# Top-p attention and adjacency on one core: sums from counts, two adj accumulators, layer 1's weights in two pieces

## The chip, the cores and the metric

The kernel runs on one core of a Trainium2 chip. The metric is the device time of that core, in microseconds (us); lower is better. The core has five engines with instruction streams of their own: TensorE (PE in the profile; its weight loads are PEld), VectorE (DVE), ScalarE (ACT), GpSimd (POOL), and SyncE (SP), which here only issues DMAs. They meet through semaphores. Each engine works through its stream in order.

## The reference, cut to what matters

There are N = 3327 nodes with 256 features; `adj` is a sparse random matrix with weights, held dense. Two layers follow each other; only the first concerns us closely.

```python
h  = relu(layernorm(x))
R  = (adj + I) / rowsum
for n in range(2):                      # two propagation steps
    A  = top_p(softmax(q @ k.T), 0.9)   # q, k: 64 wide, from Xa
    Xf = R @ Xf
    Xa = A @ Xa
    Z  = Z + Xf @ U1[n].T + Xa @ U2[n].T
x  = x + layernorm(h + Z) * g + b
# layer 1: attention over neighbours (4 heads of 64), masked by adj > 0
x  = x + elu(softmax(mask(leaky_relu(s_i + d_j))) @ (relu(layernorm(x)) @ W))
```

`top_p` keeps, in each row, the largest probabilities until they sum to 0.9, and sets the others to zero. Put the other way: it drops the smallest entries whose sum stays below 0.1 of the row's sum.

## The kernel before, in words

The 3327 rows make 26 tiles of 128 rows (NT = 26). Layer 0 goes through two propagation steps (n = 0 and n = 1, called the first and the second step here). Per step and row tile there are two streams of work.

**Attention rows** (class `Row`, pieces put by `search` and `attention`). Logits come from TensorE (L842), their exponentials from ScalarE (L853), which leaves a row of 3327 float32 numbers `e` in SBUF. Then the threshold is sought without a sort. A guess t0 comes from the row's moments. At a threshold t the kernel needs twice the sum of all entries below t, called B, and compares it with b, a tenth of the row's sum. `count` (L890) makes it with two passes of ScalarE over the row: Relu(t - e) summed gives `r0`, Sign(t - e) summed gives `s0` (the number below less the number above), and B = (s0 + N) t - 2 r0. `step` (L904 and after) takes B, estimates the density near t and moves to the next threshold by a damped Newton step; it is a string of some fifteen operations on one number per row, on GpSimd for the first two thresholds. The first step of propagation uses two thresholds, the second three (`EVALS`). At the third, VectorE makes the sum in one pass (`sum_below`, L936) and also does the `step`. After it VectorE takes the largest entries below the last threshold (`window`, L947 and L952), sorts them and finds the exact cut (`sort`, `choose`), and sets what is below it to zero (`drop`, L1002). A window of 24 or 32 entries must hold the cut; `least` is a guard that opens the window fully when few entries are left above the threshold. TensorE then transposes the row, 128 columns at a time (L1015), ScalarE copies the transposes to SBUF (`et`, L1020), and TensorE multiplies them with Xa into the accumulator `acca` (L1027).

**Adjacency tiles** (class `Full`, put by `full`). 26 blocks of adj come by DMA into `at` buffers (L1047) and are multiplied on TensorE into one accumulator `accf` in PSUM (L1053), two blocks to a planned piece. ScalarE copies the result out (`copy`, L1060), and VectorE adds it up (`add`, L1069 and after). There is one accumulator, so tile t+1 can't begin before the copy of tile t.

**Layer 1's weights** (`layer1_weights`, L700): four loads and eight VectorE operations, in one piece put with `plan.put("DVE", 3.0, base + NT - 1.0, layer1, needs=[used], lag=3.0)`. It needs only the first projections (`used`). Two tiles of the `et` pool, which has three, hold its data; the planner isn't told of these.

**The order of the work** is set by a planner written in the kernel, `Plan` (L470 and after). Every piece of work has an engine, an assumed length, a rank, needs (pieces that must be done), and buffers that it takes and gives. `order` plays the pieces through on assumed clocks: whenever an engine is free, it starts the ready piece of lowest rank whose buffers are free. Each engine's stream stands in that order, for good; on the chip the engines follow it and wait on semaphores where the data aren't there. A wait that the planner doesn't know of, or a length that it assumes too short, doesn't change the order. The ScalarE copies of accumulators have rank -90 and so come as early as ScalarE is free in the plan. `Row.count` on ScalarE is assumed to take 3.05, `Row.step` on GpSimd 3.8 and 4.7, `sum_below` on VectorE 3.65.

Layer 1 (`attend_neighbours`) follows from about 1775 us on and is not touched; its two kinds of accumulators use the PSUM space of `acca` and `accf`.

Of the kernel before, what the change touches and what calls it, by code (L numbers as in the profile page):

```python
# [10 lines left out]
F32 = mybir.dt.float32  # L11
BF16 = mybir.dt.bfloat16
I32 = mybir.dt.int32
U16 = mybir.dt.uint16
AF = mybir.ActivationFunctionType
ALU = mybir.AluOpType
# [3 lines left out]
P = 128  # L20
N = 3327
NT = 26
NP = NT * P
D = 256
# [7 lines left out]
BIG = 3.0e38  # L32
# [13 lines left out]
WIN = (24, 32)  # L46
# [6 lines left out]
BUFS = dict(kk=2, e=4, sc=6, f=3, xa=2, xt=2, kq=3, ystage=2, base=1, mv=4, cum=2)  # L53
# [517 lines left out]
def fast(  # L571
# [18 lines left out]
    V, S, T, GP = nc.vector, nc.scalar, nc.tensor, nc.gpsimd  # L590
# [35 lines left out]
    with ExitStack() as l0:  # L626
# [3 lines left out]
        scr = l0.enter_context(tc.tile_pool(name="scr", bufs=1))  # L630
# [3 lines left out]
        ps_a = l0.enter_context(tc.tile_pool(name="ps_a", bufs=1, space=PSUM))  # L634
# [62 lines left out]
                for r in range(2):  # L697
                    S.copy(wqk[:, k, r, (1 - r) * DA : (2 - r) * DA], ps)

        def layer1_weights():  # L700

            late = wpool.tile([P, 2 * D + 2 * (H * FH + 2 * H)], F32, name="late")
            g_all, b_all = late[:, :D], late[:, D : 2 * D]
            wa = late[:, 2 * D :].rearrange("p (c o) -> p c o", c=2)
            a_all = etpool.tile([P, H, 2 * FH], F32, name="et")
            nc.sync.dma_start(g_all, ln_g.partition_broadcast(P))
            nc.sync.dma_start(b_all, ln_b.partition_broadcast(P))
            nc.sync.dma_start(a_all, gat_a.partition_broadcast(P))
            nc.sync.dma_start(wa[:, :, : H * FH], gat_w.rearrange("(c p) o -> p c o", p=P))
            prod = etpool.tile([P, 2, H, FH], F32, name="et")  # L710
            for k in range(2):
                for a in range(2):
                    V.tensor_mul(
                        prod[:, 0],
                        wa[:, k, : H * FH].rearrange("p (h f) -> p h f", h=H),
                        a_all[:, :, a * FH : (a + 1) * FH],
                    )
                    lo = H * FH + a * H
                    V.tensor_reduce(wa[:, k, lo : lo + H], prod[:, 0], AX.X, ALU.add)
            return g_all, b_all, wa  # L720

        def moments(t, kq, ps_k, ps_g):

# [84 lines left out]
            a = plan.put("ACT", 0.6, rank, exps, needs=[a])  # L808
            return plan.put("DVE", 0.6, rank, rest, needs=[a])

        plan = Plan(dict(pl=2, px=2, acca=1, accf=1, et=3, at=4, y=1, e2=2, mask=2, **BUFS))

        class Row:


            NAMES = (
                "b v w t0 t1 t2 u g k2 p0 p1 p2 p3 j0 j1 j2 j3 r0 s0 B0 B1 B2 q d dt least up h0 h1 room K zs nxt cnt m "
                "tk rec".split()
            )

# [64 lines left out]
            def count(self, k, fn):  # L885

                junk = scr.tile([P, NP], mybir.dt.float8e5, name="junk")
                dst = (self.r0, self.s0)[fn == AF.Sign]
                t = (self.t0, self.t1, self.t2)[k]
                S.activation(junk[:, :N], self.e[:, :N], fn, bias=t, scale=-1.0, accum_out=dst, saturate=False)  # L890

            def step(self, k, eng):

                TS, TT = eng.tensor_scalar, eng.tensor_tensor
                t, tn, B = (self.t0, self.t1, self.t2)[k], (self.t1, self.t2, self.up)[k], (self.B0, self.B1, self.B2)[k]
                last = k + 1 == EVALS[self.n]

                def invert(x):
                    if eng is V:
                        V.reciprocal(x, x)  # L900
                    else:
                        TT(x, x, powers[:, 2:3], ALU.pow)

                if k < 2:  # L904
                    TS(self.q, self.s0, float(N), t, ALU.add, ALU.mult)  # L905
                    TS(B, self.r0, -2.0, self.q, ALU.mult, ALU.add)
                else:
                    TS(B, B, 2.0, None, ALU.mult)
                TS(self.d, B, -0.5, self.b, ALU.mult, ALU.add)
                if k == 0:  # L910

                    TS(self.g, self.u, cs[:, self.i : self.i + 1], 0.25, ALU.mult, ALU.min)
                    TS(self.least, self.s0, N - 2.0 * (WIN[self.n] - 2), BIG, ALU.is_ge, ALU.mult)
                    TS(self.least, self.d, 0.0, self.least, ALU.is_ge, ALU.mult)
                else:
                    TT(self.u, B, (self.B0, self.B1)[k - 1], ALU.subtract)
                    TT(self.w, self.k2, self.g, ALU.mult)
                    TS(self.w, self.u, self.dt, self.w, ALU.mult, ALU.add)
                    TS(self.v, self.u, self.u, self.k2, ALU.mult, ALU.add)
                    invert(self.v)  # L920
                    TT(self.g, self.w, self.v, ALU.mult)
                TS(self.q, self.g, 0.5, 1.0 / AIM[self.n], ALU.mult, ALU.add)
                invert(self.q)
                TS(self.d, self.q, t, self.d, ALU.mult, ALU.add)  # L924
                TT(self.d, self.d, self.g, ALU.mult)
                if last:
                    TS(self.d, self.d, t, self.least, ALU.add, ALU.max)
                    TS(self.up, t, 0.25, self.d, ALU.mult, ALU.max)  # L928
                else:
                    TT(self.d, self.d, t, ALU.add)  # L930
                    TS(tn, t, 0.25, self.d, ALU.mult, ALU.max)  # L931
                    TS(self.dt, tn, t, 2.0, ALU.subtract, ALU.mult)

            def sum_below(self):
                y = scr.tile([P, NP], BF16, name="y")
                V.scalar_tensor_tensor(  # L936
                    y[:, :N], self.e[:, :N], self.t2, self.e[:, :N], ALU.is_lt, ALU.mult, accum_out=self.B2
                )

            def window(self, a, part):  # L940

# [95 lines left out]
        class Full:  # L1037


            def __init__(self, n, t):  # L1040
                self.n, self.t, self.at = n, t, {}
                self.src, self.w = (main, D + 1) if n == 0 else (c, D)

            def load(self, q):
                m = min(JC, NT - q * JC)
# [2 lines left out]

            def some(self, js):
                for j in js:  # L1050
                    if j == 0:
                        self.acc = ps_a.tile([P, D + 1], F32, name="accf")
                    T.matmul(  # L1053
                        self.acc[:, : self.w], self.at[j // JC][:, j % JC, :], self.src[:, j, : self.w],
                        start=(j == 0), stop=(j == NT - 1),
                    )
# [286 lines left out]
        def search(row, rank, keys, stats_of, fresh):  # L1343


            n, i = row.n, row.i
            got, a = [], None
# [14 lines left out]
            a = plan.put("ACT", 0.35, rank - 2.4, row.row_sum, needs=[got])  # L1362
# [1 line left out]
            a = row.pieces["guess"] = plan.put("ACT", 1.0, rank - 2.4, row.guess, needs=[a])  # L1364
            more = plan.put("ACT", 0.85, rank - 2.05, row.density, needs=[a])
            for j in range(2):
                got = [plan.put("ACT", 3.05, rank - (2.1, 1.7)[j], row.count, j, fn, needs=[a]) for fn in (AF.Relu, AF.Sign)]
                a = plan.put("POOL", (3.8, 4.7)[j], rank - (2.0, 1.6)[j], row.step, j, GP, needs=[got, more])
            if EVALS[n] == 3:
                a = plan.put("DVE", 3.65, rank - 1.3, row.sum_below, needs=[a], take=["y"], give=["y"], lag=0.02, hold=3.6)  # L1370
                a = plan.put("DVE", 2.7, rank - 1.3, row.step, 2, V, needs=[a])
            halves = []
            for h in range(2):
# [33 lines left out]
        def full(n, t, rank, right, after):  # L1407

            f = Full(n, t)
            loads = [  # L1410
                plan.put("SP", 0.1, rank, f.load, q, needs=[after], take=["at"], lag=3.3) for q in range(-(-NT // JC))
            ]
            loaded[0] = loads[-1]
            a = None
            for j in range(0, NT, 2):
                last = j % JC == JC - 2 or j == NT - 2
                a = plan.put(
                    "PE", 0.437 * 2, rank, f.some, range(j, j + 2), needs=[a, loads[j // JC], right[j : j + 2]],
                    take=["accf"] * (j == 0), give=["at"] * last,
                )  # L1420
            a = plan.put("ACT", 0.3, -90.0, f.copy, needs=[a], take=["f"], give=["accf"])
            if n == 1:
                b = plan.put("SP", 0.1, rank, f.fetch, needs=[loads[-1], stored[t]], take=["base"], lag=3.0)
                return plan.put("DVE", 0.88, -90.0, f.add, needs=[a, b], give=["f", "base"], hold=0.85)
            return plan.put("DVE", 1.15, -90.0, f.add, needs=[a], give=["f"])
# [229 lines left out]
        layer1_ready = None  # L1655
        sources = [project_u(t, -1.9 + 0.001 * t) for t in range(NT)]
        right, fresh, failed = None, None, []
        for n in range(STEPS):
            base = 30.0 * n
# [21 lines left out]
            if n == 0:  # L1681
# [13 lines left out]
                used, sources = sources, [(p,) for p in fulls]  # L1695

                def layer1():
                    late["g"], late["b"], late["wa"] = layer1_weights()

                layer1_ready = plan.put("DVE", 3.0, base + NT - 1.0, layer1, needs=[used], lag=3.0)  # L1700
            else:
                ends = [finish2(r, done[r.i], fulls[r.i], base + r.i + 0.2) for r in rows]
        attend_neighbours(rows, ends, done, fulls)
# [62 lines left out]
```

## Time and profile before

The time is the median of three runs.

| | |
|---|---|
| time, median (lowest to highest) | 2310.74 us (2310.22 to 2312.15) |
| span of the profiled run, clock | 2307.9 us, 0.988 |
| ScalarE counts, L890 | 208 x 3072 ns, and 191 ns each to read the sum |
| VectorE sums at the third threshold, L936 | 26 x 3672 ns, and 83 ns each |
| adj matmuls, L1053 | 1352 x 383 ns (first step), 1352 x 388 ns (second step) |
| copy of the adj accumulator, L1060 | 52 x 368 ns |
| layer 1's weights on VectorE, L713 and L719 | 4 x 425 ns, 4 x 420 ns |

In time: up to about 120 us the inputs are read and projected; the first step runs to about 970 us, the second to about 1775 us, and layer 1 to the end. Lines of the profile give a group of instructions by source line, engine and operation; a wait is written as who waited, then after an arrow for whom, with the total in us, the number of times, and the longest. In a list in order of time the brackets hold the idle time of that engine before the instruction, and what ended it. Idle time of an engine that doesn't set the end costs nothing.

### The profile page before, as it was taken

The page shows a single profiled execution, that of the slowest core. Times are in us where ns is not written, and L with a number is a line of the kernel's source. Part 1 is how long each engine was busy: PE and PEld are TensorE (multiplying, and loading weights), DVE is VectorE, ACT ScalarE, POOL GpSimd, SP SyncE. Part 2 cuts the span into 40 slices and gives each one's busy share as a digit, 9 for nine tenths or more (in the row PEclk, how much of TensorE's full clock was granted, in tenths as well). Part 3 has the DMA queues.
Part 4 walks back from the last instruction along what each step waited for, and adds up shares of the span by engine and source line. Part 5 has one row for each costly group of instructions (what it writes and reads, how often), then busy time and mean ns, then how long its engine had stood idle before and what let it go on. Part 6 is the DMA issues. An engine that isn't in the chain of part 4 may idle for free. (4 is left out here: it accounts for less than half of the span.)

```text
span 2307.9 us, 36154 instructions
## 1 busy us (share of the span) xinstructions
PE 2223.0 (96%) x11956; PEld 1551.9 (67%) x11956; DVE 1699.8 (74%) x4299; ACT 1559.9 (68%) x2901; POOL 1017.6 (44%) x2263
## 2 busy tenths in 40 slices
PE   7989999999999999999999999999998999999997
PEld 5467777777877778777777778777877434333332
DVE  5564666656645664389889889889888797989895
ACT  5767788678777862488676787777773556565553
POOL 6345455445554541357766765677774000000000
PEclk9999999999999999999999999999999999999998
DMA  3021212212212222522212222122223343434341
GB/s 97 1 68 52 68 54 60 64 53 61 73 47 72 68 87 73 176 85 65 65 51 68 68 76 67 53 62 68 71 67 99 90 114 109 116 99 127 100 130 42
DMA packets 189654, 176.97 MB, mean 77 GB/s; under 512 B 14866, under 2 KB 145808, under 8 KB 189328
## 3 DMA queue, kind: packets, MB, share of 16 engines
q1 hardware_dynamic: 187472, 173.30, 25.8%
q8 instruction: 96, 1.57, 0.3%
q10 hardware_dynamic: 1984, 1.26, 0.2%
q14 instruction: 102, 0.84, 0.1%
HBM read 157.66 MB, written 15.89 MB: 75 GB/s over the span
## 5 line engine op out<-in xcount | busy, mean ns | idle before, releaser
L890 ACT ACTIVATE junk<-e,sc 128x3327 fp8e5<-128x3327 f32 x208 | 638.9, 3072 | 25.4 <-POOL sc L931 23.4
L1027 PE MATMUL acca<-rhs,et 128*128 128x256 f32 x2704 | 623.6, 381 | 2.3 <-ACT et L1020 2.2
L1027 PEld LDWEIGHTS acca<-rhs,et 128*128 128x128 f32 x2704 | 500.6, 191 | 66.9 <-ACT et L1020 4.8
L1053 PE MATMUL accf<-c,at 128*128 128x256 f32 x1352 | 322.8, 388 | 20.4 <-ACT f L1060 20.3
L947 DVE SCALAR_TENSOR_TENSOR y<-e,sc 128x1664 f32<-128x1664 f32 x104 | 204.6, 1967 | 187.0 <-POOL sc L928 169.3
L1053 PE MATMUL accf<-main,at 128*128 128x257 f32 x1352 | 317.0, 383 | 4.8 <-DMA at<-in_adjt_dram 4.5
L1020 ACT COPY et<-px 128x512 f32<-128x512 f32 (+1 forms) x364 | 194.4, 554 | 186.4 <-PE acca L1027 125.3
L1053 PEld LDWEIGHTS accf<-c,at 128*128 128x128 f32 x1352 | 251.6, 192 | 78.4 <-ACT f L1060 28.8
L1522 DVE SCALAR_TENSOR_TENSOR e<-c,low,et 128x832 f32<-128x832 f32 x288 | 289.1, 1075 | 16.8 <-ACT e L1592 9.5
L1053 PEld LDWEIGHTS accf<-main,at 128*128 128x128 f32 x1352 | 250.9, 191 | 46.4 <-issue 8.0
L952 DVE MAX8 cands<-y 128x8 f32<-128x208 f32 x832 | 241.1, 361 | 3.6
L1002 DVE SCALAR_TENSOR_TENSOR e<-e,thr 128x832 f32<-128x832 f32 x208 | 214.0, 1083 | 2.6 <-ACT kq L1178 0.5
L1538 PE MATMUL pl<-e,main 128*64 128x416 f32 x1152 | 212.6, 516 | 0.1
L1015 PE MATMUL px<-ident,e 128*128 128x128 f32 x1352 | 196.4, 277 | 16.8 <-ACT et L1020 7.9
L853 ACT ACTIVATE e<-pl 128x1024 f32<-128x1024 f32 x208 | 179.3, 865 | 45.6 <-PE pl L842 44.7
L1015 PEld LDWEIGHTS px<-ident,e 128*128 128x128 f32 x1352 | 163.4, 143 | 57.5 <-issue 13.6
L1511 ACT ACTIVATE et<-at 128x512 bf16<-128x512 f32 (+1 forms) x208 | 114.5, 550 | 118.3 <-DVE e L1522 76.9
L842 PE MATMUL pl<-kt,qq 64*128 64x512 f32 (+1 forms) x728 | 184.1, 588 | 0.0
L905 POOL TENSOR_SCALAR sc<-sc 128x1 f32<-128x1 f32 x104 | 40.2, 386 | 309.3 <-ACT junk L890 249.3
L1538 PEld LDWEIGHTS pl<-e,main 128*64 128x64 f32 x1152 | 79.6, 137 | 123.1 <-issue 104.0
L936 DVE SCALAR_TENSOR_TENSOR y<-e,sc 128x3327 bf16<-128x3327 f32 x26 | 95.5, 3672 | 47.9 <-POOL sc L931 47.9
L1522 DVE SCALAR_TENSOR_TENSOR rhs<-c,low,et 128x832 f32<-128x832 f32 x128 | 129.2, 1073 | 0.0
(485 smaller groups left out, 3076.8 us busy)
## 6 DMA issues: line engine op xcount, KB each, us to landing
at<-in_adjt_dram SPq DMA_DIRECT2D x416, 256.0 KB, 2.8
at<-in_adjt_dram SPq DMA_DIRECT2D x104, 192.0 KB, 3.0
at<-in_adjt_dram SPq DMA_DIRECT2D x52, 128.0 KB, 2.1
ys<-ystage SPq DMA_DIRECT2D x26, 256.0 KB, 2.4
rhs<-in_x_dram SPq DMA_DIRECT2D x26, 128.0 KB, 3.3
ystage<-in_x_dram SPq DMA_DIRECT2D x26, 128.0 KB, 2.1
base<-ys SPq DMA_DIRECT2D x26, 128.0 KB, 2.2
x1s<-ystage SPq DMA_DIRECT2D x26, 128.0 KB, 1.7
```

The source lines that it names most:

```text
L842: T.matmul(pl[:, r, :m], qq[half, self.i, :], kt[half, 512 * k : 512 * k + m], start=True, stop=True,)
L853: S.activation(self.e[:, 1024 * k : 1024 * k + pl.shape[1]], pl, AF.Exp, accum_out=(self.p0, self.p1, self.p2, self.p3)[k],)
L890: S.activation(junk[:, :N], self.e[:, :N], fn, bias=t, scale=-1.0, accum_out=dst, saturate=False)
L947: V.scalar_tensor_tensor(self.y[:, : hi - lo], self.e[:, lo:hi], self.up, self.e[:, lo:hi], ALU.is_lt, ALU.mult, accum_out=(self.h0, self. ...
L952: V.max(self.cands[:, o // PIECE, :], self.y[:, o - lo : min(o + PIECE, hi) - lo])
L1002: V.scalar_tensor_tensor(piece, piece, self.thr[:, o : o + 1], piece, ALU.is_gt, ALU.mult)
L1015: T.transpose(pt[:, k, :], self.e[:, j * P : (j + 1) * P], ident)
L1020: S.copy(self.et[g][:, :m, :], self.pt.pop(g)[:, :m, :])
L1027: T.matmul(self.acc, et[:, j - 4 * g, :], rhs[self.n][:, j, :], start=(j == 0), stop=(j == NT - 1))
L1053: T.matmul(self.acc[:, : self.w], self.at[j // JC][:, j % JC, :], self.src[:, j, : self.w], start=(j == 0), stop=(j == NT - 1),)
L1522: V.scalar_tensor_tensor(held["e"][:, k, :], extra["both"][b % 2][:, k, :], low[:, j, k : k + 1], held["mask"], ALU.max, ALU.mult,)
L1538: T.matmul(q["acc"][a][k * FH : (k + 1) * FH, c, :C], main[:, j, h * FH : (h + 1) * FH], held["e"][:, h, c * C : (c + 1) * C], start=(j == 0),
```

## The change

It has three parts.

**Sums from counts.** Between two neighbouring thresholds t_(k-1) and t_k lie (s_k - s_(k-1)) / 2 entries; each is taken to be worth the mean of the two thresholds. So twice the sum changes by (s_k - s_(k-1)) (t_k + t_(k-1)) / 2, and only the Sign count is needed at the second and third threshold. The Relu pass at the second threshold goes in both steps, and the VectorE pass at the third is replaced by a Sign pass on ScalarE. The counts need columns of their own (`s0 s1 s2`). The guard `least` is computed at threshold k = n instead of always at the first.

**Two adj accumulators in the second step.** One PSUM tile of 2 x 256 float32 numbers holds two accumulators; tiles of even and odd number take them in turn. The planner knows them as `accf0` and `accf1`, and holds `accf` itself for the whole step.

**Layer 1's weights in two pieces.** The loads are a piece on the DMA queue that needs row 3's attention to be done and takes an `et` buffer; the VectorE operations are a second piece that needs the loads and takes another.

```diff
-        def layer1_weights():
+        def layer1_loads():
...
+            return g_all, b_all, wa, a_all
+
+        def layer1_scores(wa, a_all):
+
             prod = etpool.tile([P, 2, H, FH], F32, name="et")
...
-                dst = (self.r0, self.s0)[fn == AF.Sign]
+                dst = (self.s0, self.s1, self.s2)[k] if fn == AF.Sign else self.r0
...
-                if k < 2:
-                    TS(self.q, self.s0, float(N), t, ALU.add, ALU.mult)
+                s = (self.s0, self.s1, self.s2)
+                if k == 0:
+                    TS(self.q, s[0], float(N), t, ALU.add, ALU.mult)
                     TS(B, self.r0, -2.0, self.q, ALU.mult, ALU.add)
                 else:
-                    TS(B, B, 2.0, None, ALU.mult)
+                    TS(self.q, t, (self.t0, self.t1)[k - 1], 0.5, ALU.add, ALU.mult)
+                    TS(self.u, s[k], s[k - 1], self.q, ALU.subtract, ALU.mult)
+                    TT(B, (self.B0, self.B1)[k - 1], self.u, ALU.add)
                 TS(self.d, B, -0.5, self.b, ALU.mult, ALU.add)
+                if k == self.n:
+
+                    TS(self.least, s[k], N - 2.0 * (WIN[self.n] - 2), BIG, ALU.is_ge, ALU.mult)
+                    TS(self.least, self.d, 0.0, self.least, ALU.is_ge, ALU.mult)
                 if k == 0:
-
                     TS(self.g, self.u, cs[:, self.i : self.i + 1], 0.25, ALU.mult, ALU.min)
-                    TS(self.least, self.s0, N - 2.0 * (WIN[self.n] - 2), BIG, ALU.is_ge, ALU.mult)
-                    TS(self.least, self.d, 0.0, self.least, ALU.is_ge, ALU.mult)
                 else:
-                    TT(self.u, B, (self.B0, self.B1)[k - 1], ALU.subtract)
...
-                    if j == 0:
+                    if j == 0 and self.n == 0:
                         self.acc = ps_a.tile([P, D + 1], F32, name="accf")
+                    elif j == 0:
+
+                        if self.t == 0:
+                            late["accf"] = ps_a.tile([P, 2, D], F32, name="accf")
+                        self.acc = late["accf"][:, self.t % 2, :]
...
-                got = [plan.put("ACT", 3.05, rank - (2.1, 1.7)[j], row.count, j, fn, needs=[a]) for fn in (AF.Relu, AF.Sign)]
+                got = [
+                    plan.put("ACT", 3.05, rank - (2.1, 1.7)[j], row.count, j, fn, needs=[a])
+                    for fn in (AF.Relu, AF.Sign)[j:]
+                ]
                 a = plan.put("POOL", (3.8, 4.7)[j], rank - (2.0, 1.6)[j], row.step, j, GP, needs=[got, more])
             if EVALS[n] == 3:
-                a = plan.put("DVE", 3.65, rank - 1.3, row.sum_below, needs=[a], take=["y"], give=["y"], lag=0.02, hold=3.6)
+                a = plan.put("ACT", 3.05, rank - 1.4, row.count, 2, AF.Sign, needs=[a])
                 a = plan.put("DVE", 2.7, rank - 1.3, row.step, 2, V, needs=[a])
...
-                    take=["accf"] * (j == 0), give=["at"] * last,
+                    take=[f.bank] * (j == 0) + ["accf"] * (n == 1 and t + j == 0), give=["at"] * last,
                 )
-            a = plan.put("ACT", 0.3, -90.0, f.copy, needs=[a], take=["f"], give=["accf"])
+            a = plan.put(
+                "ACT", 0.3, -90.0, f.copy, needs=[a], take=["f"],
+                give=[f.bank] + ["accf"] * (n == 1 and t == NT - 1),
+            )
...
-                layer1_ready = plan.put("DVE", 3.0, base + NT - 1.0, layer1, needs=[used], lag=3.0)
+                a = plan.put("SP", 0.5, base + 4.0, layer1, needs=[used, done[3]], take=["et"], lag=8.0)
+                layer1_ready = plan.put(
+                    "DVE", 3.7, base + 5.0, lambda: layer1_scores(late["wa"], late["a"]), needs=[a], take=["et"],
+                    give=["et", "et"],
+                )
```

More of the change, by code (lines that the diff above doesn't have):

```diff
@@ L719, in layer1_weights @@
                     V.tensor_reduce(wa[:, k, lo : lo + H], prod[:, 0], AX.X, ALU.add)
-            return g_all, b_all, wa
         def moments(t, kq, ps_k, ps_g):
@@ L809, in stats @@
             return plan.put("DVE", 0.6, rank, rest, needs=[a])
-        plan = Plan(dict(pl=2, px=2, acca=1, accf=1, et=3, at=4, y=1, e2=2, mask=2, **BUFS))
+        plan = Plan(dict(pl=2, px=2, acca=1, accf=1, accf0=1, accf1=1, et=3, at=4, y=1, e2=2, mask=2, **BUFS))
         class Row:
             NAMES = (
-                "b v w t0 t1 t2 u g k2 p0 p1 p2 p3 j0 j1 j2 j3 r0 s0 B0 B1 B2 q d dt least up h0 h1 room K zs nxt cnt m "
+                "b v w t0 t1 t2 u g k2 p0 p1 p2 p3 j0 j1 j2 j3 r0 s0 s1 s2 B0 B1 B2 q d dt least up h0 h1 room K zs nxt cnt m "
                 "tk rec".split()
@@ L932, in step @@
                     TS(self.dt, tn, t, 2.0, ALU.subtract, ALU.mult)
[L934 to L938, printed above, removed]
             def window(self, a, part):
@@ L1042, in __init__ @@
                 self.src, self.w = (main, D + 1) if n == 0 else (c, D)
+                self.bank = f"accf{t % 2}" if n else "accf"
             def load(self, q):
@@ L1697, in layer1 @@
                 def layer1():
-                    late["g"], late["b"], late["wa"] = layer1_weights()
-                layer1_ready = plan.put("DVE", 3.0, base + NT - 1.0, layer1, needs=[used], lag=3.0)
+                    late["g"], late["b"], late["wa"], late["a"] = layer1_loads()
+                a = plan.put("SP", 0.5, base + 4.0, layer1, needs=[used, done[3]], take=["et"], lag=8.0)
[3 more added lines that the diff above has]
+                )
             else:
```

## The prediction

> **What bounds the kernel now.** I read the page's busy times and its forty slices first, then the stretches of the two propagation steps, then TensorE's waits in the second step, and last the order in time around its longest gaps.
>
> ```profile
> PE 2223.0 (96%) x11956; PEld 1551.9 (67%) x11956; DVE 1699.8 (74%) x4299; ACT 1559.9 (68%) x2901; POOL 1017.6 (44%) x2263
> ...
> PEclk9999999999999999999999999999999999999998
> ```
>
> TensorE sets the time; whatever is won must be TensorE idle time, or time at a reduced clock. Idle altogether: 2307.9 - 2223.0 = 85 us. The stretches say where (columns: length; then busy time of TensorE, its weight load, VectorE, ScalarE, GpSimd; then the clock):
>
> ```profile
> 100.00:150.00 50.00, 40.03 (x156) 25.45 (x157) 36.50 (x129) 35.26 (x60) 19.68 (x54) 0.93 0.12 37
> ...
> 150.00:800.00 650.00, 648.41 (x3195) 509.59 (x3193) 383.61 (x1137) 499.59 (x827) 337.26 (x802) 1.00 0.21 61
> 1000.00:1750.00 750.00, 726.03 (x3550) 582.82 (x3549) 654.78 (x1885) 563.98 (x953) 530.76 (x1068) 0.99 0.23 67
> ```
>
> The body of the first step (150 to 800) has 1.6 us of idle: nothing can be won there. The body of the second has 24 us, with VectorE at 87% against 59% in the first. Before 150 us another 10 us are idle. TensorE's waits from 970 to 1775 us:
>
> ```profile
> PE accf L1053 <- ACT f L1060: 20.3, 17, 5.1
> PE px L1015 <- DVE e L1002: 2.9, 4, 2.3
> PE acca L1027 <- ACT et L1020: 0.8, 1, 0.8
> ```
>
> So in the second step TensorE waits nearly always for one thing: ScalarE's copy that empties the adj accumulator (L1060). The longest such wait, in order of time on four engines:
>
> ```profile
> 1448.11 3.69 DVE L936 SCALAR_TENSOR_TENSOR y<-e,sc 128x3327 bf16<-128x3327 f32 x1 [6.74 <-POOL sc L931]
> 1448.17 3.79 POOL L932 TENSOR_SCALAR sc<-sc 128x1 f32<-128x1 f32 x1
> 1458.17 3.07 ACT L890 ACTIVATE junk<-e,sc 128x3327 fp8e5<-128x3327 f32 x1 [1.88 <-POOL sc L931]
> 1472.26 0.35 ACT L1060 COPY f<-accf 128x256 f32<-128x256 f32 x1
> 1472.66 2.07 PE L1053 MATMUL accf<-c,at 128*128 128x256 f32 x4 [5.13 <-ACT f L1060]
> ```
>
> VectorE's long pass (L936) starts, a GpSimd scalar operation that normally takes 0.3 us (median 315 ns) lasts 3.79 us, ScalarE gets its thresholds late, and the accumulator's copy stands in ScalarE's queue behind four counts. The gap near the start is another matter:
>
> ```profile
> 126.67 0.43 DVE L713 TENSOR_TENSOR et<-late,et 128x256 f32<-128x256 f32 x1 [5.74 <-DMA late<-in_gat_w_dram]
> 129.87 1.09 ACT L1020 COPY et<-px 128x512 f32<-128x512 f32 x2 [5.39 <-DVE et L713]
> 130.50 1.11 PE L1015 MATMUL px<-ident,e 128*128 128x128 f32 x4 [5.32 <-ACT et L1020]
> ```
>
> Layer 1's weights are loaded and multiplied in one planned piece on VectorE, which sits on the load with two of three `et` buffers held: TensorE stands 5.32 us.
>
> **What the Trainium skill says.** "PSUM — Partial Sum Buffer", section on bank collisions: two engines on one bank and the same partitions collide even at disjoint columns, and the hardware doesn't arbitrate, so the program must keep them apart. No collision is in this trace; the waits for L1060 are such an ordering. "Perfetto Trace Analysis", Optimizing Tensor Performance, advises independent matmul groups to rotate through different banks. "SBUF — State Buffer", Who interferes with whom: a VectorE instruction with two SBUF inputs contends with a GpSimd instruction that reads SBUF. The trace agrees: 3.79 us beside L936's 3.69. "TensorE: Matmul & The Clock Gate", Part 1: after about 3.4 us of idling TensorE runs at half rate until it has been busy as long. The trace agrees: after the 5.13 us gap four adj matmuls take 2.07 us, where four take 1.03 elsewhere; the 50 us stretch around it has a clock of 0.93.
>
> **Layer 1's weights in two pieces.** The loads now wait until row 3's attention is done, go out on the sync queue, and the eight VectorE operations (4 x 425 + 4 x 420 ns = 3.4 us) follow as a separate piece with the buffers counted. In the compiled order they land while TensorE has 20 adj matmuls to run (20 x 0.383 = 7.7 us). Won: 5.3 us, and the half-rate stretch after it: four transposes in 1.11 us instead of 0.60, eight attention matmuls in 3.62 instead of 1.89, 2.2 us in all. I take 8; 5 to 10 with the small `et` waits of 0.7 around it.
>
> **Counts instead of sums.** Per row and threshold a count costs ScalarE 3072 + 191 ns = 3.26 us. First step: 26 fewer, 85 us less ScalarE; hidden, since TensorE is already full there. Second step: 26 Relu counts out, 26 Sign counts at the third threshold in: ScalarE unchanged. VectorE loses 26 x (3672 + 83 ns) = 98 us and gets back one or two scalar operations per row (0.2 us, 5 us together): 655 of 750 falls to about 565. What TensorE sees of it: the 2.9 us waits for L1002 (I take 2), and fewer GpSimd operations held up for 3.7 us, hence a ScalarE closer to its plan.
> Against it stands a new wait. The third count waits for the second GpSimd step, where VectorE used to wait (47.9 us in 12 of 26 rows) with little behind it. In ScalarE's strict order the copies for attention and adjacency are queued behind the count. An undisturbed second step ran from 1464.62 to 1469.96 us when its threshold was ready, 5.3 us; the two `least` operations move into it (0.23 and 0.29 plus gaps, 0.7 us): 6.0. The plan has 4.7 + 0.1. So the count is up to 1.2 us late per row, 31 us of ScalarE. ScalarE has room (564 of 750), TensorE only the work ahead of it. Bounds 0 and 31 us; I take a quarter, 8, because ScalarE's waits for GpSimd now (11.4 us in 11 cases) left TensorE waiting only 0.8 us for `et`.
>
> **Two accumulators.** They are two halves of one 2 KB bank. In the compiled program the copy of tile t waits for the matmuls of tile t+1 that stand before it, and those behind it wait for the copy: the halves aren't independent. What changes is the plan, which no longer sees a wait. Of 25 tile changes, 13 have the copy in the middle of the next tile; 8 of these have nothing else for TensorE there, 5 have transposes or logits. The other 12 have attention or logits between the tiles. Per bare change the wait is at least 0.46 us (the shortest now, copy 0.37 plus handshakes), and (20.3 - 5.1)/16 = 0.95 us when ScalarE is as late as now: 4 to 8 us, plus 1 for the five. I take 7 of 20.3; the gain is 13 (between 0 and 20). Of the clock loss at 1150, 1350 and 1450 us, (0.03 + 0.03 + 0.07) x 50 = 6.5 us, 4 come back.
>
> **The end of the second step.** The last adj tile now ends behind the last attention. Before, TensorE idled 7 us from 1775 to 1807 over `sd` and `et` waits of 0.2 to 4.2 us; without the attention among them some remain. I take 2 us won, between +4 lost and 5 won.
>
> **Sum.** -8 - 2 + 8 - 13 - 4 - 2 = -21: 2290 us.
>
> **The rivals.**
> - Full gain: the third count comes in time and the tile changes are filled. 8 + 2.9 + 20.3 + 6.5 + 5 = 43: 2268. For it: VectorE at 75% as in no stretch of this step now, and GpSimd freed of 26 holds. Against: the shared bank.
> - Renamed waits: the accumulator's wait turns into others of the same size, and only the weights' gain stays: 2303. For it: ScalarE's order is where all waits end, and its work in that step doesn't fall.
> - Slower: the late third count costs TensorE its whole bound, +31, against 8 for the weights and a halved accumulator gain of about 10: 2324. For it: strict order, and 0.1 us of slack in the plan. Against: ScalarE has been late already without `et` waits.
>
> **How the numbers follow.** Forecast 0.50, full gain 0.20, renamed 0.18, slower 0.12. The range 2266 to 2309 holds the first three and leaves out the slower case, with a few per cent beyond the full gain. Faster than 2306: 0.48 + 0.20 + 0.13 = 0.81; within 0.2%: 0.07; slower: 0.12.
>
> **What would show it.** Right: no `et` wait of 5 us before 150 us and its clock above 0.95; no L936; GpSimd's longest threshold operation near 2 us instead of 3.8; TensorE's wait for the adj copy 5 to 10 us, in the middle of tiles; ScalarE waiting for GpSimd's L931 successor more than 11 us. The first step's body must keep its 2 us of idle. Wrong: adj waits still near 20 us, or `et` waits of over 10 us in the second step.

## The result, and the profile after

The changed kernel takes 2271.99 us (median of four runs, 2270.80 to 2272.88) against 2310.6 us for the kernel before (four runs here, three further up): a ratio of 0.9831, with a 95% interval of 0.9814 to 0.9848. That is 38.6 us less, where 21 were forecast.

Three marks in the two traces divide the gain: the first adj matmul of the second step, the first product of layer 1, and the end of the span. Before they stand at 972.8, 1807.4 and 2307.9 us; after at 957.5, 1771.5 and 2269.9 us. So 15.3 us were won up to the first mark, 20.6 between the first and the second (834.6 became 814.0), and 2 in layer 1. The marks are single instructions in an order that changes too, so they are good to a few us only; the times of whole runs decide below.

The busy times and the granted clock on the page of the changed kernel:

```profile
PE 2207.6 (97%) x11956; PEld 1547.5 (68%) x11956; DVE 1618.2 (71%) x4273; ACT 1480.0 (65%) x2849; POOL 915.3 (40%) x2263
...
PEclk9999999999999999999999999999999999999998
```

TensorE is busy 15.4 us less at the same 11956 matmuls, in part because the clock was granted at 0.992 instead of 0.988, and idle 62 us instead of 85. VectorE lost the 26 long sums, ScalarE 26 passes net. GpSimd is busy 102 us less with the same number of instructions, 2263. The same three stretches as before (length; busy time of TensorE, weight load, VectorE, ScalarE, GpSimd; clock):

```profile
100.00:150.00 50.00, 47.15 (x211) 31.73 (x211) 35.39 (x134) 38.02 (x75) 31.55 (x68) 1.00 0.04 10
150.00:800.00 650.00, 648.57 (x3207) 511.05 (x3207) 398.51 (x1169) 444.80 (x793) 326.75 (x822) 1.00 0.22 64
1000.00:1750.00 750.00, 738.95 (x3659) 598.81 (x3658) 607.48 (x1939) 563.81 (x960) 444.00 (x1062) 1.00 0.24 67
```

The stretch before 150 us runs 211 matmuls instead of 156, at full clock. The body of the first step was full and stays full. In the second step the idle time fell from 24 to 11 us, ScalarE does what it did (564 us), and GpSimd's busy time fell from 531 to 444 us at nearly the same number of instructions (1068 and 1062). TensorE's waits from 970 to 1775 us:

```profile
PE accf L1060 <- ACT f L1067: 4.4, 9, 0.9
PE px L1016 <- ACT et L1021: 4.2, 4, 2.4
PE px L1289 <- ACT c L1477: 2.7, 1, 2.7
PE px L1473 <- ACT c L1477: 2.3, 2, 2.2
PE px L1016 <- DVE e L1003: 1.9, 4, 0.7
```

The wait for the adj copy, 20.3 us before, is 4.4 here and never longer than 0.9. It looks like the work of the second accumulator. The experiments say it isn't.

### The profile page after: what moved, and what is told of

The parts are those of the page before. It is cut to its first block, busy times and chain, and to the rows that moved or that the text cites. A ratio compares the mean times of both kernels' runs of the same rounds, so it can differ in the third digit from the quotient of the medians.

```text
span 2269.9 us, 36125 instructions
## 1 busy us (share of the span) xinstructions
PE 2207.6 (97%) x11956; PEld 1547.5 (68%) x11956; DVE 1618.2 (71%) x4273; ACT 1480.0 (65%) x2849; POOL 915.3 (40%) x2263
## 5 line engine op out<-in xcount | busy, mean ns | idle before, releaser
L893 ACT ACTIVATE junk<-e,sc 128x3327 fp8e5<-128x3327 f32 x182 | 559.1, 3072 | 59.1 <-POOL sc L938 57.8
L1060 PE MATMUL accf<-c,at 128*128 128x256 f32 x1352 | 313.4, 382 | 4.8 <-ACT f L1067 4.7
L845 PEld LDWEIGHTS pl<-kt,qq 64*128 64x128 f32 x728 | 70.9, 185 | 82.3 <-issue 76.5
L1523 ACT ACTIVATE at<-at 128x512 f32<-128x512 f32 (+1 forms) x208 | 112.1, 539 | 4.3 <-DMA at<-in_adjt_dram 4.2
```

The lines of the kernel that those rows point to most:

```text
L845: T.matmul(pl[:, r, :m], qq[half, self.i, :], kt[half, 512 * k : 512 * k + m], start=True, stop=True,)
L1060: T.matmul(self.acc[:, : self.w], self.at[j // JC][:, j % JC, :], self.src[:, j, : self.w], start=(j == 0), stop=(j == NT - 1),)
```

## The experiments

"Adj wait" below is TensorE's wait for the copy of the adj accumulator over the whole run (before: 20.6 us), and "second step" is the time between the first two marks (before: 834.6 us).

### Which part brings the gain

Two theories stood against each other. A: the two accumulators bring it, as the prediction had it. H: the sums from counts bring it, because VectorE's long two-input pass no longer holds up GpSimd. Each part was made alone, and then all without the accumulators.

**Layer 1's weights in two pieces alone.** The rest is as before.

```diff
-                layer1_ready = plan.put("DVE", 3.0, base + NT - 1.0, layer1, needs=[used], lag=3.0)
+                a = plan.put("SP", 0.5, base + 4.0, layer1, needs=[used, done[3]], take=["et"], lag=8.0)
+                layer1_ready = plan.put(
+                    "DVE", 3.7, base + 5.0, lambda: layer1_scores(late["wa"], late["a"]), needs=[a], take=["et"],
...
```

> Only layer 1's weights in two pieces, the rest as before. Both theories: the 5.3 us wait near 127 us and the half clock after it go, and nothing else. By the two traces, 14 us lie before the second step begins. Theory W (all of it is the weights): 2297. Rival: the weights are worth only the wait and its clock, 8 us, and the other 6 are due to fewer counts on ScalarE: 2302.5. The second step keeps its length and its 20 us of waits for the adj copy.

Measured: 2300.0 us, ratio 0.9964 (0.9951 to 0.9976), 9.1 us under the 2309.1 of the kernel before on that chip. The first mark comes at 962.4, 10.4 us earlier; the second step is unchanged (834.1). Its adj wait is also unchanged:

```profile
PE accf L1056 <- ACT f L1063: 20.4, 18, 5.1
```

**Two accumulators alone.**

```diff
-                    take=["accf"] * (j == 0), give=["at"] * last,
+                    take=[f.bank] * (j == 0) + ["accf"] * (n == 1 and t + j == 0), give=["at"] * last,
...
-            a = plan.put("ACT", 0.3, -90.0, f.copy, needs=[a], take=["f"], give=["accf"])
+            a = plan.put(
+                "ACT", 0.3, -90.0, f.copy, needs=[a], take=["f"],
+                give=[f.bank] + ["accf"] * (n == 1 and t == NT - 1),
+            )
```

> Only the two adj accumulators. Theory H (the gain of the second step comes from VectorE's long pass, which held GpSimd and made ScalarE late): the shared bank leaves the wait in place, and the time falls by at most 5 us: 2306. Theory A (the order that the planner makes with two accumulators is what frees TensorE): 2295, and the waits for the adj copy fall from 20 us to about 5.

Measured: 2303.21 us, ratio 0.9975 (0.9967 to 0.9982), 5.9 us less. TensorE's two largest waits of that kernel:

```profile
PE px L1015 <- ACT et L1020: 16.9, 15, 4.8
PE accf L1059 <- ACT f L1066: 8.4, 18, 0.9
```

The adj wait falls by 12 us, close to the 13 of the forecast. But the wait for the transposes' copies (`et`) grows from 7.9 to 16.9 us: 6.1 us of it lie between 970 and 1740 us, where there was none, and 4.4 after 1740 us (1.0 before). The adj tiles run ahead (the last adj matmul starts at 1721 us, before at 1774), and attention rows are left for the end, 44 matmuls of them even behind the second mark, which is why that mark is not used for this kernel. Most of what the second accumulator wins is lost again in these waits.

**Sums from counts alone.**

```diff
-                got = [plan.put("ACT", 3.05, rank - (2.1, 1.7)[j], row.count, j, fn, needs=[a]) for fn in (AF.Relu, AF.Sign)]
+                got = [
+                    plan.put("ACT", 3.05, rank - (2.1, 1.7)[j], row.count, j, fn, needs=[a])
+                    for fn in (AF.Relu, AF.Sign)[j:]
+                ]
...
-                a = plan.put("DVE", 3.65, rank - 1.3, row.sum_below, needs=[a], take=["y"], give=["y"], lag=0.02, hold=3.6)
+                a = plan.put("ACT", 3.05, rank - 1.4, row.count, 2, AF.Sign, needs=[a])
```

> Only the sums from counts. Theory H: the second step gains some 16 us, waits for the adj copy under 10 us, GpSimd operations no longer held for 3.7 us: 2292, or 2288 if the first step also gains from ScalarE. Theory A: the waits for the adj copy stay near 18 us: 2306.

Measured: 2275.17 us, ratio 0.9856 (0.9840 to 0.9873), 33.9 us less. First mark 960.6, second step 812.3. One accumulator, and yet:

```profile
PE accf L1051 <- ACT f L1058: 6.0, 10, 1.9
```

**Counts and weights, one accumulator.** The changed kernel without the accumulators' edits above.

> The changed kernel with one adj accumulator as before. Theory H: 2277, five more than the changed kernel. Theory A: 2287, with waits for the adj copy near 18 us.

Measured: 2271.27 us, ratio 0.9839 (0.9823 to 0.9856); adj wait 5.7 us in 9 cases; second step 812.3. The changed kernel with all three parts, run again as a yardstick for the later runs (no edit):

> The changed kernel itself, on the same chip as the next three. 2272, against which they are read; the kernel with all counts and one accumulator stood at 2271.

Measured: 2272.11 us (2270.61 to 2273.36), ratio 0.9837 (0.9824 to 0.9851). With one accumulator and with two the time is the same. A falls: beside the counts the accumulators are worth nothing. Of H this shows that the counts bring the gain, not yet by what. The three gains alone, 9.1 + 5.9 + 33.9 = 48.9 us, overlap: the counts by themselves also shorten the gap near 130 us (the longest `et` wait before 150 us is 1.8 us there, 5.3 before), since the order around it changes.

### Why the counts bring it

H says only that the long pass is bad. All kernels below are the last one (counts and weights, one accumulator) with one thing put back or added. Two readings of H: P, the VectorE pass does the harm, through what it holds or through its length; S, ScalarE's load does it, and the Relu at the second threshold was the harm.

**The third sum by VectorE again** (no Relu at the second threshold). ScalarE makes three counts per row, VectorE the long pass. In this edit `hold` tells the planner how long the pass holds up GpSimd; the plan lengthens GpSimd's pieces by it. So the plan of the kernel before knew of these holds.

```diff
...
-                a = plan.put("ACT", 3.05, rank - 1.4, row.count, 2, AF.Sign, needs=[a])
+                a = plan.put("DVE", 3.65, rank - 1.3, row.sum_below, needs=[a], take=["y"], give=["y"], lag=0.02, hold=3.6)
```

> Weights in two pieces, one adj accumulator, the Relu count at the second threshold dropped, but the sum at the third threshold made by VectorE's long pass as before. Against the kernel with all counts and one accumulator (2271 us). Theory P (the long pass on VectorE made the second step slow): the 22 us of the second step come back nearly whole, 2291; the start stays as fast. Theory S (ScalarE's load counts): here ScalarE has 26 passes fewer than with all counts, so the second step is as fast or faster, 2266 to 2271.

Measured: 2268.99 us, ratio 0.9829 (0.9813 to 0.9845); adj wait 5.1; second step 808.1.

**The Relu at the second threshold kept in both steps** (no VectorE pass). ScalarE makes five counts per row in the second step.

```diff
...
-                    for fn in (AF.Relu, AF.Sign)[j:]
+                    for fn in (AF.Relu, AF.Sign)
```

> Weights in two pieces, one adj accumulator, the third threshold by a Sign count, but the Relu count at the second threshold kept in both steps, so ScalarE has 26 passes more in each step (85 us each). Theory P: the second step keeps its gain, the first is full anyway, at most the start loses some 4 us: 2276. Theory S: ScalarE at 645 of 740 us makes its copies late, the second step loses its gain: 2290.

Measured: 2292.08 us, ratio 0.9933 (0.9916 to 0.9949); first mark 963.9 (7 us later than without), second step 826.9 (14.6 more). Its adj wait:

```profile
PE accf L1058 <- ACT f L1065: 20.6, 16, 3.7
```

**The long pass added, its result unused.** Four counts on ScalarE, and VectorE's two-input pass beside them.

```diff
+            def extra(self):
+                y = scr.tile([P, NP], BF16, name="y")
+                V.scalar_tensor_tensor(
+                    y[:, :N], self.e[:, :N], self.t2, self.e[:, :N], ALU.is_lt, ALU.mult, accum_out=self.K
+                )
...
-                a = plan.put("ACT", 3.05, rank - 1.4, row.count, 2, AF.Sign, needs=[a])
+                x_ = plan.put("DVE", 3.65, rank - 1.3, row.extra, needs=[a], take=["y"], give=["y"], lag=0.02, hold=3.6)
+                a = [x_, plan.put("ACT", 3.05, rank - 1.4, row.count, 2, AF.Sign, needs=[a])]
```

> All counts, one adj accumulator, and VectorE's long pass added back at the third threshold as work whose result is not used; the next step waits for it and for the count. It has two SBUF inputs and makes GpSimd stand. Theory P, by the hold on GpSimd: as slow as with the sums, 2288. Theory P, by VectorE's time: also 2288; the next run tells the two apart. Theory S: 2271 to 2275.

**The same with a pass of one input**, of nearly the same length (3595 ns against 3680), at the same place in the plan (its `hold` too is kept there); its result is unused too.

```diff
+            def extra(self):
+                V.tensor_reduce(self.K, self.e[:, :N], AX.X, ALU.max)
```

> As the run before, with the same plan, but the extra VectorE pass is a maximum over the row: one SBUF input, some 3.5 us by the row of the small maxima (128x128 in 0.29 us). If the hold on GpSimd is the cause, GpSimd's operations keep their 0.3 us beside it and the time is 2274. If VectorE's time is the cause, 2288.

Measured: with two inputs 2285.42 us, ratio 0.9898 (0.9881 to 0.9914); with one 2271.14, ratio 0.9837 (0.9821 to 0.9854). The stretch from 1000 to 1740 us in three kernels, first the one with the two-input pass:

```profile
1000.00:1740.00 740.00, 717.39 (x3499) 577.58 (x3500) 658.43 (x1875) 556.49 (x934) 533.53 (x1048) 0.99 0.23 67
```

then the one with the one-input pass:

```profile
1000.00:1740.00 740.00, 726.84 (x3583) 587.63 (x3582) 671.26 (x1908) 559.89 (x945) 447.44 (x1053) 1.00 0.24 68
```

and the one with three counts and VectorE's sum at the third threshold:

```profile
1000.00:1740.00 740.00, 729.92 (x3603) 591.30 (x3602) 674.55 (x1918) 488.43 (x897) 542.96 (x1056) 1.00 0.24 69
```

The first two differ in one VectorE pass per row; in the two traces TensorE, ScalarE, VectorE and GpSimd work through everything else in the same order. VectorE is as busy in both (658 and 671 us), ScalarE too (556 and 560); only GpSimd's busy time differs, 534 against 447 us, at the same work: with the two-input pass its small operations stand still. That is 14.3 us of run time, and 829.1 against 810.7 us for the second step. "SBUF — State Buffer" of the Trainium skill, in Who interferes with whom, says that a VectorE instruction with at most one SBUF input, outside the two-port modes, doesn't contend with GpSimd; this pair agrees. That the two-input pass writes a row and the maximum doesn't is not the reason: the one-input pass further down writes the same row, and GpSimd is busy 434 us beside it. How holds reach TensorE shows in the kernel with the two-input pass, at its longest adj wait, in order of time on GpSimd, ScalarE and TensorE:

```profile
1114.77 3.56 POOL L672 TENSOR_SCALAR mv<-mv 128x1 f32<-128x1 f32 x1 [4.68 <-DVE mv L667]
...
1138.50 2.26 POOL L938 TENSOR_SCALAR sc<-sc 128x1 f32<-128x1 f32 x1
...
1140.79 3.07 ACT L893 ACTIVATE junk<-e,sc 128x3327 fp8e5<-128x3327 f32 x1 [3.49 <-POOL sc L938]
1143.85 0.35 ACT L1067 COPY f<-accf 128x256 f32<-128x256 f32 x1
1144.10 1.07 ACT L1027 COPY et<-px 128x512 f32<-128x512 f32 x2
...
1144.26 2.07 PE L1060 MATMUL accf<-c,at 128*128 128x256 f32 x4 [3.60 <-ACT f L1067]
```

In the first line the extra pass holds a small GpSimd operation for 3.56 us. Later a count waits 3.49 us for GpSimd's threshold, the copies stand behind the count, and TensorE behind the copies. The hold that makes this wait stands right in front of it: GpSimd's last three operations before the count took 0.95, 0.92 and 2.26 us, and the same three took 0.19, 0.19 and 0.30 us with the one-input pass. They ran beside `drop` (L1009), four VectorE passes with two inputs (4.07 us together) that every kernel here has. With the one-input pass GpSimd was through 0.5 us before `drop` began; with the two-input pass GpSimd stood 1.5 us further back against VectorE and met it. So the long pass did harm here by making GpSimd late for another hold; which of its earlier holds did that is open. That holding GpSimd costs the 14 us is shown by the pair. The sum of the waits doesn't foretell it: ScalarE's waits for GpSimd from 1000 to 1740 us add up to 41.7 us with the two-input pass and 14.2 with the one-input pass, but to 41.0 in the changed kernel, where TensorE waits 3.9 us for the adj copy.

The third of the stretches is held just as much (543 us) and is the fastest of all. Put together ("held" means by the long pass; `drop` is in every row):

| counts per row on ScalarE, second step | GpSimd held | adj wait | run |
|---|---|---|---|
| 3 | yes | 5.1 us | 2268.99 us |
| 4 | no | 5.7 us | 2271.27 us |
| 4, and a one-input pass | no | 9.1 us | 2271.14 us |
| 4, and a two-input pass | yes | 17.0 us | 2285.42 us |
| 4, kernel with the weights alone | yes | 20.4 us | 2300.0 us |
| 5 | no | 20.6 us | 2292.08 us |
| 3, and a one-input count on VectorE (below) | no | 9.7 us | 2286.93 us |

P and S each fit a part. In the first six rows the adj copy comes late when ScalarE has four counts and waits for a held GpSimd, or has five, and lifting either load alone brings the time to about the same level (2269 and 2271 us). The last row doesn't fit. Only the pair of extra passes keeps the order of the work; in every other row the planner made another order together with the edit. So the harm of the hold is shown, in one order; that ScalarE's load does as much by itself is argued. VectorE's busy time as such is not it: 671 and 675 us of 740 go with the fast runs.

### The late third count

**The planner told of longer steps on GpSimd.** The prediction had charged 8 us because the third count would stand late in ScalarE's queue.

```diff
-                a = plan.put("POOL", (3.8, 4.7)[j], rank - (2.0, 1.6)[j], row.step, j, GP, needs=[got, more])
+                a = plan.put("POOL", ((4.4, 4.7), (3.8, 6.0))[n][j], rank - (2.0, 1.6)[j], row.step, j, GP, needs=[got, more])
```

> All counts, weights in two pieces, one adj accumulator, and the planner told the length of GpSimd's steps as the trace shows them: 4.4 and 4.7 in the first propagation step, 3.8 and 6.0 in the second, instead of 3.8 and 4.7. If the late third count costs TensorE what the prediction took for it, 8 us: 2264. If ScalarE's waits for GpSimd are hidden: 2271, with fewer of them (54.8 us now).

Measured: 2274.78 us, ratio 0.9850 (0.9835 to 0.9865): no gain, rather 3 us more. ScalarE's wait for the threshold over the whole run, first with the plan's old lengths, then with the new:

```profile
ACT junk L893 <- POOL sc L938: 54.8, 33, 6.1
```

```profile
ACT junk L893 <- POOL sc L938: 28.3, 16, 3.9
```

Half of the waiting went and little came of it: between the two marks TensorE is idle 14.9 us instead of 15.8, and its adj wait even rose from 5.7 to 9.2 us. Most of ScalarE's waits must lie where TensorE has other work. The new order loses in front: up to the first mark TensorE is idle 32.7 us instead of 28.5, since one wait of 4.9 us for VectorE appears there. The edit changed the lengths for both steps, so the run as a whole can't price the third count; the idle time of the second step can.

### Both loads lifted, and a miss

**The third count on VectorE with a one-input pass.** If each relief is enough, both together should do no worse: three counts on ScalarE and no long pass that holds. One small operation more per row turns the number below into what Sign gives.

```diff
+                    if k == 2:
+                        TS(self.s2, self.s2, 2.0, float(N), ALU.mult, ALU.subtract)
...
+            def count_below(self):
+                y = scr.tile([P, NP], BF16, name="y")
+                V.tensor_scalar(y[:, :N], self.e[:, :N], self.t2, 0.0, ALU.is_lt, ALU.add, accum_out=self.s2)
...
-                a = plan.put("ACT", 3.05, rank - 1.4, row.count, 2, AF.Sign, needs=[a])
+                a = plan.put("DVE", 3.6, rank - 1.3, row.count_below, needs=[a], take=["y"], give=["y"], lag=0.02)
```

> One adj accumulator, weights in two pieces, and the Sign count at the third threshold made on VectorE: a compare with one SBUF input that adds up as it goes. So ScalarE has three passes per row and GpSimd is not held, both at once. If either relief is enough, nothing more is to be had: 2267 to 2270, as with VectorE's sum (2269). If the two add up: 2262.

Measured: 2286.93 us, ratio 0.9898 (0.9883 to 0.9913). A miss. With the longer GpSimd lengths of the run before as well (its edit and this one):

> The last one with the lengths of GpSimd's steps told right. If the planner's errors about GpSimd still cost anything: 2262. If not: as the run before.

Measured: 2294.91 us, ratio 0.9936 (0.9923 to 0.9950), slower still. As with these lengths before, the loss lies in front (first mark 965.4 against 958.9); the second step is as long as in the run before (827.0 and 828.0), though its adj wait is 17.1 us. In the first of the two no long pass holds GpSimd, and ScalarE is little loaded:

```profile
1000.00:1740.00 740.00, 718.84 (x3529) 579.52 (x3529) 673.04 (x1930) 486.50 (x893) 434.26 (x1051) 0.99 0.23 66
```

A sample of what is lost, in order of time:

```profile
1366.99 0.22 POOL L672 TENSOR_SCALAR mv<-mv 128x1 f32<-128x1 f32 x1 [2.13 <-DVE mv L667]
...
1376.29 1.89 POOL L941 TENSOR_SCALAR sc<-sc 128x1 f32<-128x1 f32 x1
...
1379.57 0.29 ACT L876 ACTIVATE sc<-sc,adds 128x1 f32<-128x1 f32 x1 [6.84 <-POOL sc L871]
...
1381.65 1.11 PE L1022 MATMUL px<-ident,e 128*128 128x128 f32 x4 [4.87 <-ACT et L1027]
```

VectorE delivers late, GpSimd follows, and its last three operations of the step before are held by `drop` once more (0.86, 1.34 and 1.89 us). ScalarE waits 6.84 us for the next row's first threshold with the `et` copy behind it, and TensorE waits 4.87. So a chain over the first threshold does here what the other chain did there. But VectorE is as busy in the fastest kernel (675 us), so its load alone is no cause. The order is the untested rival: this pass was planned without `hold`, so the planner made another order than for VectorE's sum. The same pass in that order, as in the pair above, would part the two; it was not run, and the cause stays open. No version beats the changed kernel clearly: the one with VectorE's sum is 3 us below it (0.9829 against 0.9831 and 0.9837), inside the intervals.

## Why the prediction was right and where it failed

The time lay in the range, but 18 us from the forecast and nearest to the rival called full gain (2268). That it lay in the range is luck as far as the mechanism goes: the range is 43 us wide, and the largest term was booked on the wrong part. Full gain wasn't foretold for the right reason either, since it has the third count in time. The sum, term by term:

- **Weights, -8: right.** Alone they are worth 9.1 us, in front of the first mark, as said: the `et` wait of 5.3 us is gone and the clock before 150 us is 1.00.
- **The Relu of the first step, 0 because "TensorE is already full there": too small.** It is full from 150 us on, not before. With the weights mended but the Relu kept, ScalarE is busy 43 of the 50 us from 100 to 150 and TensorE runs 198 matmuls; without the Relu it is busy 38, and TensorE runs 214. The first mark moves from 962.4 to 956.8 (957.4 in the kernel with VectorE's sum, where as many matmuls stand in front of it), and is at 963.9 with the Relu restored: some 5 us or a little more.
- **"fewer GpSimd operations held up for 3.7 us, hence a ScalarE closer to its plan", priced within a -2: this step failed.** The mechanism was named and even shown at the longest gap, but the gain was booked on the accumulators. The counts alone shorten the second step by 22.3 us. The pair of extra passes shows that the hold can cost most of this (829.1 against 810.7 us). VectorE fell to 607 us in the body of that step, not to 565; nothing was priced on that.
- **The late third count, +8: too much.** It comes late as foreseen (ScalarE's waits for L938 are 57.8 us, for L931 before they were 23.4), but halving these waits took only 0.9 us off TensorE's idle time in the second step. What the other half costs was not measured.
- **Two accumulators, -13, and the clock, -4: wrong owner.** The adj wait fell to 4.9 us over the run, just under the 5 to 10 given, but it falls to 5.7 without them. What was said of the two halves, that they aren't independent, held: alone, a wait of 8.4 us in 18 short pieces remains, and 9 us appear elsewhere. The clock came back with one accumulator too (1.00 instead of 0.99 in the body of the second step), when the long waits went.
- **The end of the second step, -2: right.** 2.7 and 2.3 us of waits are left there of 7; with one accumulator they are 3.1 and 2.2.

In the second step the terms gave -13 (-2 +8 -13 -4 -2), and 20.6 were won. The other tell-tales came out as written: no `et` wait of 5 us before 150 us; the first step's body keeps its 1.4 us of idle; and GpSimd's last threshold operation, 3.79 us at its longest before, is at most half of that (from 1000 to 1740 us; shortest, median and longest in ns):

```profile
L939 POOL TENSOR_SCALAR sc<-sc x48: 297/302/1864, 1008.1 to 1700.8; 128x1 f32<-128x1 f32 x48
```

They couldn't part the accumulators from the counts, since both foretell a short adj wait.

## What to carry to other kernels

A wait names the buffer that came late, not the reason: before a second buffer is bought, ask what stands in front of the copy in its engine's queue, and try relieving that alone. Two loads on one queue can do harm together and little singly, so gains of parts don't add up; nor is relief of both sure to be as good as of one. Of two edits that explain the same wait only a run with one of them tells which did it. To price one cause, keep the order and change one instruction, as the pair of extra passes does. In a stream ordered ahead by assumed lengths, relief at one place can give an order that loses elsewhere, so an edit is judged by its run.

## What was not expected of the hardware

A VectorE pass over 128 x 3327 float32 takes nearly the same time in three forms: 3680 ns with two inputs, 3669 ns comparing one input with a column and summing, 3595 ns as a maximum. Of these only the first holds GpSimd (534 us busy from 1000 to 1740 us, against 434 and 447 at nearly the same work). The short two-input passes of `drop` hold it too: operations of 0.2 to 0.3 us took up to 2.26 us beside them. Two accumulators in one PSUM tile made 18 waits for the copy of 0.47 us each (8.4/18, longest 0.9); one accumulator in the kernel with counts and weights made 9 of 0.63 us (5.7/9), and in sum those are less.
